# Linear attention gated by an FP4 feed-forward net: the keys' transposes in the pipeline go from TensorE to a DMA, with 16-bit halves split and joined on ScalarE

## The chip, the core and the metric

The kernel runs on one core of a Trainium2 chip. A core has a matrix engine (TensorE, PE in the profile), a vector engine (VectorE, DVE), an engine for activation functions and copies (ScalarE, ACT), a general engine (GpSimd, POOL) and an engine that issues most of this kernel's DMAs (SyncE, SP). They run side by side, each through its own list of instructions in order, and wait for each other by semaphores. Matrix products are written to PSUM, everything else on the chip is in SBUF. The metric is the time of one execution in device microseconds (us); lower is better.

## The reference

`src` has 4 batches of 2048 rows of 256 numbers, all f32. Cut to what is computed:

```python
xn = layernorm(src)                                  # over the 256 numbers of a row
q, k, v = xn @ Wq + bq, xn @ Wk + bk, xn @ Wv + bv   # 16 heads of 64
Q, K = elu(q) + 1, elu(k) + 1
KV = einsum('bshd,bshm->bhdm', K, v)                 # sum over all rows of a batch
Z = 1 / (einsum('bshd,bhd->bsh', Q, K.sum(rows)) + 1e-6)
attn = einsum('bshd,bhdm,bsh->bshm', Q, KV, Z) @ Wo + bo
x1 = layernorm(xn + attn) * g1 + be1
s = layernorm(x1 + gelu(x1 @ W1 + b1) @ W2 + b2) * g2 + be2
h = silu(fp4(xn) @ fp4(w_gate).T) * (fp4(xn) @ fp4(w_up).T)
g = silu(fp4(h) @ fp4(w_down).T)
out = src + s * g
```

`fp4` rounds blocks of 16 numbers to a small grid times a scale of the block. What matters here: KV and the sum of K need all rows of a batch before any of its rows can be finished, and the product for K needs xn with its 256 features on the partitions, that is, transposed.

## The kernel before

Rows are worked in 32 blocks of 256 (T), two tiles of 128 (TB = 2), eight blocks to a batch (NB). The 1024 columns of K are done in two halves of 512, so the keys of a batch are 16 pieces ("subs"): the first eight make the first half, each from one block of rows, and the last eight read the same rows again for the second half.

The keys of batch 0 are done ahead, in a prologue of some 200 us. Then comes the pipeline, the loop over n from line 930: block n of batch b is finished, and two subs of the keys of batch b+1 are done beside it. So in the first four blocks of a batch both subs belong to the first half. For them `keys_in` (line 403) takes the mean and variance, normalizes to xn_k on VectorE and stores it to memory (xn_d); `keys_T` (line 416) calls `keys_xnT` (line 396): four transposes of 128x128 on TensorE into one PSUM tile (pt_k), one copy from there by ScalarE to xnT_k, and a store of that to memory (xnT_d). In the last four blocks of a batch, and for the queries of the block itself, xn and its transpose are read back from there. The last batch has no keys beside it.

One pass of the loop sets this order on TensorE, which is kept as written (lines 97 to 101):

- pt_k of both subs, then pq (the queries, 32 matmuls in four PSUM tiles), pk of the first sub, pz (the denominators), pxk of the first sub (K times xn, summed over the batch), pg (gate and up, for block n+1), pd (down),
- pk of the second sub, pa (attention), pxk of the second sub, most of py (the second feed-forward product of block n-1), pt_x (transposes of x1), pscale, the rest of py, pf (the first feed-forward product of block n).

ScalarE and VectorE have no fixed order in the pipeline (line 916 ends it): a scheduler lays their instructions out when the kernel is built, and SP's too. `tc.issue_after(ins)` puts instructions behind `ins` on their engine. In order of time ScalarE does x1T (from pt_x), scaleT, m_h and m_x (for the fp4 rounding of block n+1), a table load, eight gelus from pf, the two copies of pt_k, the queries' q and e from pq with a table load among them, the keys' two ek, a table load, and the silus of pg.

The keys' chain is in `key_product` and `key_elu` (lines 425 and 440): pk on TensorE, k1 = pk + bias on VectorE, ek = exp on ScalarE, kk on VectorE, and from kk both pxk and, on GpSimd, the sum kacc.

At a block's end `spread_scales` (line 600) sends the fp4 scales by way of memory: scale_d on SP, then eight loads that spread them into qT. `grid_T` (line 617) transposes the fp4 grid, 16-bit numbers, by a DMA on SP (gridT), in two parts of 6 and 10 tiles of 128x128. `quantized_x` and `quantized_h` multiply the two in the next pass. `sums` (line 711) sends the denominators by way of memory (z_d, then four loads zb).

All PSUM tiles of single products share one pool of four ("mm", line 81). In SBUF, "e" has three buffers for the exps, "kk" three for the keys, "xn_k" and "xnT_k" three each.

Of the kernel before, what the change touches and what calls it, by code (L numbers as in the profile page):

```python
# [7 lines left out]

F32 = mybir.dt.float32
BF16 = mybir.dt.bfloat16  # L10
AF = mybir.ActivationFunctionType
ALU = mybir.AluOpType
AX = mybir.AxisListType

P = 128
# [6 lines left out]
def linear_attention_gated_by_fp4_ffn(  # L22
# [34 lines left out]
    nc = tc.nc  # L57
# [5 lines left out]
    ND = D // P  # L63
# [5 lines left out]
    TB = 2  # L69
    T = TB * P  # L70
    NB = S // T
# [6 lines left out]
    work = ctx.enter_context(tc.tile_pool(name="work", bufs=2))  # L78
# [40 lines left out]
    vector, scalar = Ordered(nc.vector), Ordered(nc.scalar)  # L119
# [40 lines left out]
    neg_one = const.tile([P, 1], F32, name="neg_one")  # L160
# [207 lines left out]
    def transposes(x, name):  # L368

        pt = mm_tile(f"pt_{name}").rearrange("p (c t) -> p c t", c=ND)  # L370
        for c in range(ND):
            for j in range(TB):
                tr(
                    pt[:, c, j * P : (j + 1) * P], x[:, j, c * P : (c + 1) * P], ident
                )
        return pt
# [4 lines left out]
    keys = {}  # L381
# [14 lines left out]
    def keys_xnT(n, xn):  # L396
        xnT = work.tile([P, ND, T], F32, tag="xnT_k", name=f"xnT_k_0_{n}", bufs=3)
        scalar.copy(xnT, transposes(xn, f"k_{n}"))
        xnT_d[n] = dram.tile([P, ND, T], F32, tag="xnT_d", name=f"xnT_d_{n}")
        nc.sync.dma_start(xnT_d[n], xnT)  # L400
        return xnT

    def keys_in(b, sub):

        f, bi = divmod(sub, NB)
        n = b * NB + bi
        if f == 0:
            keys[b, sub] = [keys_norm(n, *keys_stats(n))]
        else:
            xn = work.tile([P, TB, D], F32, tag="xn_k", name=f"xn_k_1_{n}", bufs=3)  # L410
            xnT = work.tile([P, ND, T], F32, tag="xnT_k", name=f"xnT_k_1_{n}", bufs=3)
            keys[b, sub] = [xn, xnT]
            nc.sync.dma_start(xn, xn_d[n])
            nc.sync.dma_start(xnT, xnT_d[n])

    def keys_T(b, sub):
        f, bi = divmod(sub, NB)
        if f == 0:
            keys[b, sub].append(keys_xnT(b * NB + bi, keys[b, sub][0]))

    def key_sums(b, f, tag):
        keys[b, "acc", f] = batch.tile([P, HALF], F32, tag="kacc", name=f"kacc_{b}_{f}")
# [2 lines left out]
    def key_product(xnT, f, j, nm):  # L425

        fs = slice(f * HALF, (f + 1) * HALF)
        pk = mm_tile(f"pk_{nm}_{j}")
        for c in range(ND):
            mm(  # L430
                pk, xnT[:, c, j * P : (j + 1) * P], wk_sb[:, c, fs],
                start=c == 0, stop=c == ND - 1,
            )
        k1 = work.tile([P, HALF], F32, tag="q1", name=f"k1_{nm}_{j}", bufs=3)
        vector.tensor_tensor(k1, pk, bk1[:, fs], ALU.add)
        e = work.tile([P, HALF], F32, tag="e", name=f"ek_{nm}_{j}", bufs=3)
        scalar.activation(e, k1, AF.Exp, bias=neg_one)
        return k1, e

    def key_elu(b, f, k1, e, nm, first):  # L440
# [112 lines left out]
    blk = {n: {} for n in range(NBLK)}  # L553
# [77 lines left out]
    def quantized_h(n, j):  # L631

        qh = qT[:, :NI, j * P : (j + 1) * P]
        return vector.tensor_tensor(qh, qh, gridT[n][:, j * NI : (j + 1) * NI, :], ALU.mult)
# [125 lines left out]
    def x1_T(n):  # L760
        x1 = blk[n]["x1"]
        pt = transposes(x1, f"x1_{n}")
        x1T = work.tile([P, ND, T], F32, tag="x1T", name=f"x1T_{n}", bufs=1)
        for c in range(ND):
            ins = scalar.activation(
                x1T[:, c, :], pt[:, c, :], AF.Identity,
                bias=cols["be1"][:, c : c + 1], scale=cols["g1"][:, c : c + 1],
            )
        blk[n]["x1T"] = x1T
        blk[n]["act"] = ins.ins  # L770

        nc.gpsimd.tensor_tensor(x1, x1, rows["g1"], ALU.mult)
        nc.gpsimd.tensor_tensor(x1, x1, rows["shift"], ALU.add)

    def ffn_1(n, chunks=range(NF)):
        x1T = blk[n]["x1T"]
        if "hT" not in blk[n]:
            blk[n]["hT"] = work.tile([P, NF, T], F32, tag="big", name=f"hT_{n}")
        hT = blk[n]["hT"]
        for cc in chunks[::2]:  # L780
            pf = mm_tile(f"pf_{n}_{cc}").rearrange("p (c t) -> p c t", c=2)
            for ci in range(2):
                c = cc + ci
                for d in range(ND):
                    mm(
                        pf[:, ci, :], w1_sb[:, d, c * P : (c + 1) * P], x1T[:, d, :],
                        start=d == 0, stop=d == ND - 1,
                    )
            for ci in range(2):
                c = cc + ci  # L790
                scalar.activation(
                    hT[:, c, :], pf[:, ci, :], AF.Gelu, bias=cols["b1"][:, c : c + 1]
                )

    def ffn_2(n, j, chunks=range(NF)):
        if "py" not in blk[n]:
# [25 lines left out]
    def step(gen, times=1):  # L822
        for _ in range(times):
            next(gen, None)
# [9 lines left out]
    xnT = keys_xnT(0, xn)  # L834
# [95 lines left out]
    for n in range(NBLK):  # L930
        b, bi = divmod(n, NB)
        subs = (2 * bi, 2 * bi + 1) if b + 1 < B else ()
        if n < last:
            gate = gate_up(n + 1)
        for sub in subs:
            keys_T(b + 1, sub)
        if subs:
            step(m_half)
            q_of(n)
            step(down_1)  # L940
            load_xnT(n + 1)
            kk_ins = keys_k(b + 1, subs[0])
            with tc.issue_after(kk_ins):
                ins = quantized_x(n)
            with tc.issue_after(sums(n, ins.ins).ins):
                for j in range(TB):
                    quantized_h(n, j)
            step(m_half)
            keys_xk(b + 1, subs[0])
            step(gate, 9)  # L950
            step(m_half)
            down(n, 0)
            down(n, 1)
        elif n < last:
            def values():
                quantized_h(n, 0)
                return quantized_x(n)

            step(m_half)
            q_of(n, values)  # L960
            quantized_h(n, 1)
            load_xnT(n + 1)
            down(n, 0)
            sums(n)
            step(m_half)
            step(gate, 9)
            step(m_half)
            down(n, 1)
        else:
            for j in range(TB):  # L970
                quantized_h(n, j)
                down(n, j)
        with tc.issue_after(blk[n + 1]["late"]) if n < last else nullcontext():
            qz(n)
        if subs:
            keys_k(b + 1, subs[1])
        elif n > 0:
            ffn_2(n - 1, 0, range(NF // 2))
        attention(n)
        if n + 2 < NBLK:  # L980
            load_xn(n + 2)
        if subs:
            keys_xk(b + 1, subs[1])
            if subs[1] % NB == NB - 1:
                m_half = m_of_half(b + 1, subs[1] // NB)
                step(m_half)
        bn, bin_ = divmod(n + 1, NB)
        next_subs = (2 * bin_, 2 * bin_ + 1) if bn + 1 < B else ()
        for sub in next_subs if n > 0 else ():
            keys_in(bn + 1, sub)  # L990
        if n > 0:
            ffn_2(n - 1, 0, range(0 if subs else NF // 2, NF))
            ffn_2(n - 1, 1, range(NF // 2))
        more = n + 1 < NBLK, n + 2 < NBLK
        if more[0]:
            for j in range(TB):
                scales_h(n + 1, j)
            if more[1]:
                scales_x(n + 2)
        for sub in next_subs if n == 0 else ():  # L1000
            keys_in(bn + 1, sub)
        x1_T(n)

        half_way = NF // 2 if subs else 3 * NF // 4
        if n > 0:
            ffn_2(n - 1, 1, range(NF // 2, half_way))
        if more[0]:
            spread_scales(n + 1, *more)
        if n > 0:
            ffn_2(n - 1, 1, range(half_way, NF))  # L1010
        if more[0]:
            grid_of_h(n + 1, 0)
            grid_T(n + 1, 0, NI)
            grid_of_h(n + 1, 1, blk[n]["act"])
            if more[1]:
                grid_of_x(n + 2, blk[n]["act"])
            grid_T(n + 1, NI, (NCH if more[1] else NI) * TB)
        if n > 0:
            output(n - 1)
        if n + 1 == last:  # L1020
            q_of(last)
            ffn_1(n, range(NF // 2))
            sums(last)
            ffn_1(n, range(NF // 2, NF))
        else:
            ffn_1(n)
    for j in range(TB):
        ffn_2(last, j)
        output(last, [j])
# [34 lines left out]
```

## Time and profile before

| | |
|---|---|
| median of 3 runs | 1939.84 us (1937.8 to 1939.91) |
| the profiled execution: its time, its span | 1942.96 us, 1941.1 us |
| TensorE clock granted | 0.997 |
| busy: PE, DVE, ACT, POOL | 1918.2, 1276.6, 765.2, 534.9 us |
| matmuls of pt_k: all, after 215 us | 128, 80 |
| table loads on ScalarE | 122, 156.5 us |
| DMA queue of SP: packets, data, share of the 16 DMA engines | 200008, 178.22 MB, 42.8% |

The profile is of one execution. Its span begins with the first instruction and ends with the last, and the time of the execution includes what lies around it. Durations of single instructions are latencies: matmuls overlap, so the time that a group of them holds TensorE is read from the chain of waits in order of time (start, length, engine, tile, count) and not from the mean of one. In rows of the timeline the columns are start, length, engine, line, operation, output<-inputs, shapes, count, and in brackets the idle time before and what ended it. Instructions of VectorE and ScalarE carry line 114, that of the helper that issues them, so they are told apart by their tiles.

### The profile page before, as it was taken

What the parts mean: (1) busy time and instruction counts of PE and PEld (TensorE: products, weight loads), DVE (VectorE), ACT (ScalarE), POOL (GpSimd) and SP (SyncE); (2) the same over time, 40 slices, a digit from 0 to 9 for tenths busy, and PEclk for the clock granted to TensorE, in tenths of its full rate; (3) what the DMA queues carried; (4) which work ended last, traced back from release to release, by engine and by line L of the source; (5) the groups of instructions that cost most, each with busy time, mean ns of one, the idle gap of its engine ahead of it and who ended that gap; (6) DMA issues with size and microseconds to landing.
All of it is one profiled execution on the core that took longest, in us unless ns stands there. A gap on an engine that the chain in (4) does not pass through costs nothing.

```text
span 1941.1 us, 22716 instructions
## 1 busy us (share of the span) xinstructions
PE 1918.2 (99%) x8108; PEld 1381.0 (71%) x8108; DVE 1276.6 (66%) x2300; ACT 765.2 (39%) x1340; POOL 534.9 (28%) x455
## 2 busy tenths in 40 slices
PE   9999999999999999999999999999999999999998
PEld 4446677667777677777677776677776778787786
DVE  6878656666566666666666666666565676777763
ACT  2334444334443344443343433444433443344442
POOL 4431232322233222322222323222232212222212
PEclk9999999999999999999999999999999999999999
DMA  4435445344435345444443442454533444444541
GB/s 149 144 98 120 100 93 118 83 105 91 91 59 106 94 85 107 112 91 96 89 86 71 105 104 83 89 113 93 100 80 73 75 81 86 86 82 85 90 82 41
DMA packets 200953, 181.23 MB, mean 93 GB/s; under 512 B 80101, under 2 KB 161537, under 8 KB 200841
## 3 DMA queue, kind: packets, MB, share of 16 engines
q1 hardware_dynamic: 200008, 178.22, 42.8%
q10 hardware_dynamic: 832, 1.57, 0.2%
q8 instruction: 64, 1.05, 0.2%
q14 instruction: 49, 0.39, 0.1%
HBM read 131.41 MB, written 31.54 MB: 84 GB/s over the span
## 4 chain that ended last, share of the span: by engine, by line
PE 87%; DVE 1%; DMA 1%; issue 1%; SPq 0%; POOL 0%; ACT 0%; POOLq 0%; DVEq 0%
PE pg L98 15%; PE pa L98 11%; PE pf L98 11%; PE pq L98 11%; PE py L98 11%; PE pxk L98 8%; PE pk L98 8%; PE pd L98 8%; PE pz L98 2%; PE pt_x L101 1%; PE pm L98 1%; PE pt_k L101 0%; PE pkv L98 0%; DMA zb<-z_d 0%; PE pks L98 0%
## 5 line engine op out<-in xcount | busy, mean ns | idle before, releaser
L98 PE MATMUL pg<-wgu,qT 128*128 128x352 f32 x1024 | 310.4, 461 | 0.0
L98 PEld LDWEIGHTS pg<-wgu,qT 128*128 128x128 f32 x1024 | 193.2, 190 | 118.6 <-issue 13.9
L448 POOL TENSOR_TENSOR kacc<-kacc,kk 128x512 f32<-128x512 f32 x120 | 171.8, 1432 | 298.4 <-DVE kk L114 296.4
L98 PE MATMUL pxk<-kk,xn_k 128*128 128x512 f32 x512 | 235.5, 599 | 3.3 <-DVE kk L114 3.3
L98 PE MATMUL py<-w_sb,hT 128*128 128x256 f32 x1024 | 234.5, 380 | 0.5 <-DVE s L114 0.5
L98 PE MATMUL pk<-wk_sb,xnT_k 128*128 128x512 f32 x512 | 232.1, 596 | 1.8 <-ACT xnT_k L114 1.5
L98 PE MATMUL pa<-m,zq 128*128 128x256 f32 x1024 | 228.3, 381 | 3.0 <-DVE zq L114 3.0
L98 PE MATMUL pq<-xnT,wq_sb 128*128 128x256 f32 x1024 | 228.1, 381 | 0.0
L98 PE MATMUL pf<-x1T,w_sb 128*128 128x256 f32 x1024 | 226.6, 379 | 0.0
L98 PEld LDWEIGHTS pa<-m,zq 128*128 128x128 f32 x1024 | 195.2, 191 | 41.3 <-issue 12.3
L98 PEld LDWEIGHTS py<-w_sb,hT 128*128 128x128 f32 x1024 | 191.1, 190 | 37.9 <-issue 8.1
L98 PEld LDWEIGHTS pq<-xnT,wq_sb 128*128 128x128 f32 x1024 | 194.8, 191 | 26.6 <-ACT hT L114 0.3
L98 PEld LDWEIGHTS pf<-x1T,w_sb 128*128 128x128 f32 x1024 | 194.3, 190 | 27.0 <-ACT hT L114 0.4
L677 POOL TENSOR_TENSOR o<-g,be_r 128x512 f32<-128x512 f32 x32 | 44.9, 1404 | 578.7 <-ACT g L114 578.7
L114 ACT ACT_TABLE_LOAD x122 | 156.5, 1283 | 87.1 <-DVE k L114 73.9
L114 ACT ACTIVATE x1T<-pt_x,bcol 128x256 f32<-128x256 f32 x64 | 32.6, 559 | 358.5 <-PE pt_x L101 358.5
L98 PE MATMUL pd<-wd,qT 128*128 128x256 f32 x768 | 172.3, 379 | 0.5 <-DVE qT L114 0.5
L98 PEld LDWEIGHTS pk<-wk_sb,xnT_k 128*128 128x128 f32 x512 | 97.6, 191 | 104.6 <-issue 97.0
L98 PEld LDWEIGHTS pxk<-kk,xn_k 128*128 128x128 f32 x512 | 92.5, 190 | 108.7 <-issue 80.8
L114 DVE SCALAR_TENSOR_TENSOR zq<-e,q 128x512 f32<-128x512 f32 x128 | 87.1, 689 | 124.8 <-ACT e L114 124.6
L98 PEld LDWEIGHTS pd<-wd,qT 128*128 128x128 f32 x768 | 145.8, 190 | 24.8 <-DVE qT L114 1.2
L358 POOL TENSOR_TENSOR rstd<-rstd,neg_half 128x2 f32<-128x2 f32 (+1 forms) x97 | 72.8, 751 | 316.9 <-DVE rstd L114 269.8
(121 smaller groups left out, 2324.7 us busy)
## 6 DMA issues: line engine op xcount, KB each, us to landing
zb<-z_d SPq DMA_DIRECT2D x128, 256.0 KB, 6.3
qT<-scale_d SPq DMA_DIRECT2D x248, 128.0 KB, 5.5
x_k<-in_L_attn_src_dram SPq DMA_DIRECT2D x32, 256.0 KB, 2.9
x<-in_L_attn_src_dram SPq DMA_DIRECT2D x32, 256.0 KB
xn_d<-xn_k SPq DMA_DIRECT2D x32, 256.0 KB, 3.2
xn<-xn_d SPq DMA_DIRECT2D x32, 256.0 KB, 2.6
xnT_d<-xnT_k SPq DMA_DIRECT2D x32, 256.0 KB, 5.0
xnT<-xnT_d SPq DMA_DIRECT2D x32, 256.0 KB, 2.7
```

What stands on the lines that cost most here:

```text
L98: return tc.keep_in_program_order(nc.tensor.matmul(*args, **kw))
L101: return tc.keep_in_program_order(nc.tensor.transpose(*args, **kw))
L114: ins = op(*args, **kw)
L358: nc.gpsimd.tensor_tensor(rstd[:, j0:j1], rstd[:, j0:j1], neg_half[:, j0:j1], ALU.pow)
L448: nc.gpsimd.tensor_tensor(kacc, kacc, kk, ALU.add)
L677: nc.gpsimd.tensor_tensor(o, g, rows["be2"], ALU.mult)
```

## The change

In the pipeline, from block 1 on, the keys' xn is transposed by a DMA. The DMA transpose that the kernel has, of 16-bit numbers, is used on the two halves of each f32:

- `keys_apart` sees xn_k as 16-bit numbers. Two copies on ScalarE, one for each half, of 512 numbers a partition read every second 16-bit number and write them together into `apart` (a buffer of "e"). One DMA on SP transposes its 8 tiles of 128x128 into `apartT` (a buffer of "kk").
- `keys_T` then joins them: one ScalarE copy of 1024 16-bit numbers, from apartT into xnT_k, seen as 16-bit numbers, so that each write goes to every second one. The store to xnT_d follows as before.

The places: both subs' `keys_apart` are at the end of the block before, the first one's ahead of `x1_T(n)`, the second one's behind x1T's activations. The first sub's joining is behind the last gelu of `ffn_1(n)`; the second's is moved into the next block, behind the first sub's exps. The two subs of the first block keep TensorE's transposes. The prologue is not changed.

```diff
     def keys_xnT(n, xn):
         ...
         scalar.copy(xnT, transposes(xn, f"k_{n}"))
+        store_xnT(n, xnT)
+        return xnT
+
+    def store_xnT(n, xnT):
         xnT_d[n] = dram.tile([P, ND, T], F32, tag="xnT_d", name=f"xnT_d_{n}")
         nc.sync.dma_start(xnT_d[n], xnT)
-        return xnT
...
+    def keys_apart(b, sub, issue=None):
+        f, bi = divmod(sub, NB)
+        if f > 0:
+            return
+        n = b * NB + bi
+        half = keys[b, sub][0].bitcast(U16).rearrange("p j (c f h) -> p h c j f", c=ND, h=2)
+        apart = work.tile([P, 2, ND, TB, P], U16, tag="e", name=f"apart_{n}", bufs=3)
+        with tc.issue_after(issue) if issue is not None else nullcontext():
+            for h in range(2):
+                scalar.copy(apart[:, h], half[:, h])
+        apartT = work.tile([P, 2, ND * T], U16, tag="kk", name=f"apartT_{n}", bufs=3)
+        nc.sync.dma_start(
+            apartT.rearrange("p h (m t) -> p (h m) t", t=P),
+            apart.rearrange("p h c j f -> p (h c j f)"),
+            transpose=True,
+        )
+        keys[b, sub].append(apartT)
+
-    def keys_T(b, sub):
+    def keys_T(b, sub, issue=None):
         f, bi = divmod(sub, NB)
-        if f == 0:
-            keys[b, sub].append(keys_xnT(b * NB + bi, keys[b, sub][0]))
+        if f > 0:
+            return
+        n = b * NB + bi
+        xn, *apartT = keys[b, sub]
+        xnT = work.tile([P, ND, T], F32, tag="xnT_k", name=f"xnT_k_0_{n}", bufs=3)
+        if apartT:
+            with tc.issue_after(issue):
+                scalar.copy(
+                    xnT.bitcast(U16).rearrange("p c (t h) -> p h (c t)", h=2), apartT[0]
+                )
+        else:
+            scalar.copy(xnT, transposes(xn, f"k_{n}"))
+        store_xnT(n, xnT)
+        keys[b, sub] = [xn, xnT]
...
-        scalar.activation(e, k1, AF.Exp, bias=neg_one)
+        keys["exp"] = scalar.activation(e, k1, AF.Exp, bias=neg_one).ins
...
-        for sub in subs:
+        for sub in subs if n == 0 else ():
             keys_T(b + 1, sub)
...
                 for j in range(TB):
                     quantized_h(n, j)
+            if n > 0:
+                keys_T(b + 1, subs[1], keys["exp"])
             step(m_half)
...
+        for sub in next_subs[:1]:
+            keys_apart(bn + 1, sub)
         x1_T(n)
+        for sub in next_subs[1:]:
+            keys_apart(bn + 1, sub, blk[n]["act"])
...
             ffn_1(n)
+        for sub in next_subs[:1]:
+            keys_T(bn + 1, sub, blk[n]["gelu"])
```

`ffn_1` also keeps its last gelu as `blk[n]["gelu"]`, and `blk[n]["act"]` is x1T's second activation, as before.

More of the change, by code (lines that the diff above doesn't have):

```diff
@@ L10 @@
 BF16 = mybir.dt.bfloat16
+U16 = mybir.dt.uint16
 AF = mybir.ActivationFunctionType
@@ L790, in ffn_1 @@
                 c = cc + ci
-                scalar.activation(
+                ins = scalar.activation(
                     hT[:, c, :], pf[:, ci, :], AF.Gelu, bias=cols["b1"][:, c : c + 1]
                 )
+        blk[n]["gelu"] = ins.ins
     def ffn_2(n, j, chunks=range(NF)):
```

## The prediction

> **What bounds the kernel now.** I read the page first (busy shares, then the chain of waits by engine), then the chain in order of time around single blocks.
>
> ```profile
> PE 1918.2 (99%) x8108; PEld 1381.0 (71%) x8108; DVE 1276.6 (66%) x2300; ACT 765.2 (39%) x1340; POOL 534.9 (28%) x455
> ...
> PE 87%; DVE 1%; DMA 1%; issue 1%; SPq 0%; POOL 0%; ACT 0%; POOLq 0%; DVEq 0%
> ```
>
> TensorE is busy 99% of the span and the chain is TensorE: the time is its list of matmuls, run nearly without a gap. So the question is how much list the change takes away, and where a gap opens. The chain in time, first a block whose end still has the keys' transposes (pt_k), then one that has none, because its keys' xnT is read back from memory:
>
> ```profile
> 263.63 6.91 PE pf L98 x32
> 270.54 0.87 PE pt_k L101 x8
> 271.41 6.91 PE pq L98 x32
> ```
> ```profile
> 442.76 6.91 PE pf L98 x32
> 449.67 6.91 PE pq L98 x32
> 456.57 3.43 PE pk L98 x8
> 460.00 1.00 PE pz L98 x16
> 461.01 3.63 PE pxk L98 x8
> ```
>
> With transposes pf to pq is 7.78 us, without them 6.91: eight transposes cost **0.87 us**, 109 ns each. The second block also shows that pq can follow pf directly: it is the changed kernel's order, already running. And its pxk takes 3.63 us where the block's other pxk takes 3.43 in the chain: this join (pk, VectorE's k, ScalarE's ek, VectorE's kk, pxk) already waits 0.2 us, so ScalarE running late there is paid in full.
>
> **Removed.** The pipeline transposes at the ends of blocks 0-2, 7-10 and 15-18: 11 times two tiles of four, 88 transposes. Here the view of the tile pt_k (duration min/median/max; these 80 are those after the first block, 8 more are the first block's) tempts to a larger sum:
>
> ```profile
> L101 PE MATMUL pt_k<-ident,xn_k x80: 272/273/273, 270.4 to 1277.3; 128*128 128x128 f32 x80
> L114 ACT COPY xnT_k<-pt_k x20: 584/596/607, 271.3 to 1277.9; 128x512 f32<-128x512 f32 x20
> ```
>
> 88 x 273 ns = 24.0 us. The Trainium skill says the same (TensorE: Matmul & The Clock Gate, Part 4: PE-mode transpose: about 275 ns for one in a kernel's context). But that is the latency of one; they overlap, and the chain has 0.87 us for eight. By row and rule the time would fall to 1915.8, by the chain 11 x 0.87 = **9.6 us**. I take the chain: its two differences (7.78 and 6.91) measure what TensorE is kept from. Also gone are 22 ScalarE copies of 0.6 us from PSUM, and two PSUM tiles a block.
>
> **Added on ScalarE**, per tile: two splitting copies of 512 numbers and one recombining copy of 1024. No row of before shows 16-bit copies at a stride. The nearest read SBUF and write 16 bits:
>
> ```profile
> L114 ACT ACTIVATE m_h<-h 128x704 bf16<-128x704 f32 x64 | 50.9, 796 | 46.9 <-DVE h L114 46.9
> ...
> L114 ACT ACTIVATE m_x<-y 128x512 bf16<-128x512 f32 x32 | 20.2, 632 | 5.7 <-DVE rstd L114 2.6 <-DVE y L114 2.5
> ```
>
> Slope (796-632)/192 = 0.85 ns a number: a split 0.63 us, a recombination 0.63 + 512 x 0.85 = **1.07 us**. The recombination writes every second 16-bit slot and the splits read so. Lower end: as the rows (1.07); upper end, if each half-written word costs double or more, 2.1 to 3.2 us, 2 to 3 times the row. The Trainium skill bears on it (SBUF — State Buffer, Door 1, the note on cachelines): access is at full rate while at least two accesses fall in one 16-byte line, and each step to a new line is penalised. A step of 4 bytes has four accesses in a line, so by that rule there is no penalty; no row here shows one way or the other. I take 1.07. In total ScalarE gets 22 x (2 x 0.63 + 1.07 - 0.60) = 38 us, on 765 of 1941: only its places matter.
>
> *First tile's recombination* is behind the last gelu of ffn_1. Queued behind it are the q's, whose exps feed zq, pz and the tight join. ScalarE in the block without transposes:
>
> ```profile
> 449.70 0.84 ACT L114 ACTIVATE hT<-pf,bcol 128x256 f32<-128x256 f32 x2 [0.89 <-PE pf L98]
> 451.43 0.84 ACT L114 ACTIVATE q<-pq,bcol 128x256 f32<-128x256 f32 x2 [0.89 <-PE pq L98]
> ...
> 457.88 0.72 ACT L114 ACTIVATE e<-q,neg_one 128x512 f32<-128x512 f32 x1
> 459.05 0.72 ACT L114 ACTIVATE ek<-k,neg_one 128x512 f32<-128x512 f32 x1 [0.45 <-DVE k L114]
> 461.13 0.72 ACT L114 ACTIVATE ek<-k,neg_one 128x512 f32<-128x512 f32 x1 [1.36 <-DVE k L114]
> ```
>
> Between gelu (ends 450.54) and q lie 0.89 us, and consecutive copies overlap by 0.1 us (before, two of 0.6 took 1.07). So about 1.0 us is free; from there to the last e ScalarE has no gap, and then 0.45 us before ek. A recombination up to about 1.1 + 0.45 = **1.55 us costs nothing**; every further us is a us of TensorE. At 1.07: nothing. Before, the two old copies sat there at 1.07 us as well.
>
> *Second tile's recombination* is behind the block's first two ek. Behind it wait the next table load (1.28 us) and the silu of pg. In the first block shown ScalarE idles 2.7 us there: 1.07 fits; without that cover, 1 us a block through pg's PSUM tiles.
>
> *First tile's splits* are ready when xn_k is (317 us in the block that ends at 320), in an idle stretch of 14.3 us before x1T: nothing. *Second tile's splits* come after x1T's activation, ahead of scaleT, m_h, m_x, table load and gelus: at most 1.26 us later. The first gelu would be at 325.4 instead of 324.15; TensorE needs that PSUM tile for the first pq at 329; the later gelus have 0.89 us of idle time each, so it is caught up. VectorE's grid work slips by the same 1.26 us into the 4.1 us it idles before the first zq. Nothing.
>
> **Added on SP and the DMA engines:** 22 transposes. The rows:
>
> ```profile
> L621 SPq DMA_TRANSPOSE gridT<-grid x63: 1225/1277/1967, 163.2 to 1884.9; - x63
> ...
> DMA to landing us min/median/max: 2.7/6.2/7.9
> ```
>
> New ones have 8 tiles of 128x128, the old 6 and 10: 1.3 us of issue, 2.7 (DMA engines quiet) to 7.9 us (busy) to land. First tile: copies done at 318.3, landed by 327.5 at worst, used at 329. Second: used some 20 us later. On SP the second transpose stands ahead of scale_d, 8 qT loads and the gridT transpose, and waits for the splits: scale_d goes about 2.7 us later, plus at most 1.5 us on the DMA engines. gridT, issued at 327.3 and landed by about 333.5, comes by 337.7; it is first used at 342.9, now 342.0. Hidden with 4 us to spare. The change of batch (blocks 7 and 15) has its ksum load among these too: VectorE waits 4.1 us for it until 618.06; 2.5 us more leaves some 0.6 of the 3.1 us it idles before zq: hidden, just. The second xnT_d store moves from SP's place at 331 to about 343, ahead of z_d and the four zb; zb then lands up to 1 us later, and attention has 5 us. Shared buffers (e, kk) are free in time: apart is read before the next q's, apartT goes with the recombination.
>
> **The first block** is the exception: no ffn_2 lies before ffn_1, the first gelu starts at 210.17, 4 us after its pf tile, and xn_k of the second tile is ready only at 211.6. If its splits are ahead of the gelus (208.9), these slip 2.7 + 1.26 = 4.0 us, once; if behind, some 0.7 in front of q. I take 0.7; ends 0 and 4.
>
> **Sum.** 9.6 - 0.7 = 8.9 us. The profiled execution has span 1941.1 and time 1942.96 us, so 1934.1 for a like execution; from the median of the runs, 1939.84 - 8.9 = **1931.0 us**. Within 0.2% (3.9 us) a measurement can't be told from no change.
>
> **Rivals.**
> - *The recombination is dear* (the slower side). One place: between gelu and q, 11 times. Free to 1.55 us, even at 1.55 + 8.9 / 11 = 2.4 us. At twice the row (2.14) it stalls 0.59 x 11 = 6.5 us: 1937.5. At three times (3.2) 1.65 x 11 = 18.2 us: 1949.2. For it: no row of such a copy, and the tight pxk. Against: the rows with 16-bit output keep one slope. 22%.
> - *The gain is given back by waits:* ScalarE's and SP's queues come out in another order than I laid, and a gelu, q or qT product stands 0.5 to 0.9 us a block. 11 x 0.7 = 7.7 us lost: 1938.7. For it: the order isn't written out past the named places. Against: 3 to 14 us of cover at most of them. 15%.
> - *The row's price holds:* 24 us gone, 1915.8. Against: the chain. 3%.
> - *Forecast:* 60%, its own range 1929 to 1936.
>
> Faster 0.63, same 0.15, slower 0.22. The range 1927 to 1946 takes in the first block's ends, a recombination up to some 2.9 us, and leaves out the dear end (about 0.13) and the row's price (0.03).
>
> **What would show it.** Right: pf to pq at 6.91 us in all 11 blocks, 88 transposes fewer, recombination near 1.07 us, pxk still 3.63 us. Wrong: a recombination over 1.55 us, q starting late behind it with pz and pxk longer (rival one); an idle ScalarE in front of a recombination, waiting for its DMA, or qT's product behind its loads (rival two).

## The result and the profile after

The changed kernel takes 1933.49 us (median of 9 runs, 1931.66 to 1936.48), the kernel before, run beside it, 1939.84: 6.35 us less, a ratio of 0.9966 with a 95% interval of 0.9956 to 0.9977. Two later measurements gave 0.9965 (0.9952 to 0.9977) and 0.9971 (0.9959 to 0.9983). The forecast was 8.9 us less.

The page of the changed kernel, the lines that answer to those shown of before:

```profile
PE 1906.7 (99%) x8020; PEld 1369.5 (71%) x8020; DVE 1270.7 (66%) x2300; ACT 802.9 (42%) x1384; POOL 534.5 (28%) x455
...
PE 84%; DMA 2%; DVE 1%; ACT 1%; SPq 1%; issue 0%; POOL 0%; POOLq 0%; DVEq 0%; ACTq 0%
```

88 matmuls fewer (8108 to 8020), ScalarE 38 us busier (765.2 to 802.9), TensorE as full as before. The chain's share on TensorE is 84% for 87%: in the first block the chain now runs 23 us over other engines (none before), and from block 23 on it stands on DMAs for 34 us, before for 14; in the 22 blocks between it is on TensorE alone, both times. The chain in order of time around the end of block 1, where before 0.87 us of pt_k stood between pf and pq:

```profile
263.85 6.91 PE pf L99 x32
270.76 6.91 PE pq L99 x32
277.66 3.43 PE pk L99 x8
281.10 1.00 PE pz L99 x16
282.10 3.63 PE pxk L99 x8
```

pq follows pf at once, and pk, pz and pxk have the lengths of before to the hundredth: the transposes are gone and no wait took their place. The same over the whole stretch from block 1's pf to that of block 23 (columns: stretch, length, then busy time and count of PE, PEld, DVE, ACT and POOL, TensorE's clock, DMA share, GB/s), first before, then the change:

```profile
263.60:1564.70 1301.10, 1301.10 (x5508) 940.73 (x5507) 825.77 (x1510) 522.41 (x908) 356.08 (x291) 1.00 0.44 92
```
```profile
263.80:1556.10 1292.30, 1292.30 (x5428) 932.56 (x5427) 823.20 (x1510) 555.50 (x945) 354.55 (x291) 1.00 0.46 97
```

TensorE is busy in all of it, both times; the stretch is shorter by 8.8 us for 80 matmuls fewer, 110 ns each.

So the 6.35 us are a sum of unlike parts. The start of each block's pf, read from the traces, divides the time into four stretches; the table, in us, is the key to all that follows:

| kernel | start to block 0's pf | to block 1's pf | to block 22's pf | to the end |
|---|---|---|---|---|
| before | 204.4 | 59.1 | 1242.2 | 435.5 |
| before, again | 204.5 | 59.1 | 1242.1 | 432.4 |
| the change | 203.3 | 60.4 | 1233.4 | 432.8 |
| the change, again | 203.0 | 60.4 | 1233.4 | 433.8 |
| the change, third | 202.9 | 60.4 | 1233.4 | 433.6 |

The two middle columns are the same to 0.1 us in each profile of a kernel: the first block 1.3 us longer, the 21 after it 8.8 us shorter, together some **7.4 us less** (ratio 0.9962, in all three intervals). The outer columns hold work that the change leaves alone. The last one differs by 3 us between two profiles of the same kernel. The first one, with the first loads, repeats to 0.4 us in the profiles of a kernel, but lies anywhere from 202.3 to 205.5 us in the kernels below, which do the same work up to there. The 1.1 to 1.6 us by which the change is ahead in it are there before any changed instruction runs (the second pt_k starts at 22.9 us in the one profile and at 21.8 in the other); what makes them, and whether every execution has them, is not settled. In the first pair of profiles, 11.2 us apart, both outer columns were on the change's side; the medians lie 0.3 to 1.7 us short of 7.4.

### The profile page after: what moved, and what is told of

It is laid out like the page before. It is cut to its first block, busy times and chain, and to the rows that moved or that the text cites. A ratio compares the mean times of both kernels' runs of the same rounds, so it can differ in the third digit from the quotient of the medians.

```text
span 1929.9 us, 22642 instructions
## 1 busy us (share of the span) xinstructions
PE 1906.7 (99%) x8020; PEld 1369.5 (71%) x8020; DVE 1270.7 (66%) x2300; ACT 802.9 (42%) x1384; POOL 534.5 (28%) x455
## 3 DMA queue, kind: packets, MB, share of 16 engines
q8 instruction: 63, 1.03, 0.2%
## 4 chain that ended last, share of the span: by engine, by line
PE 84%; DMA 2%; DVE 1%; ACT 1%; SPq 1%; issue 0%; POOL 0%; POOLq 0%; DVEq 0%; ACTq 0%
PE pg L99 15%; PE py L99 11%; PE pa L99 11%; PE pf L99 10%; PE pq L99 10%; PE pxk L99 8%; PE pk L99 8%; PE pd L99 8%; PE pz L99 2%; DMA qT<-scale_d 1%; PE pt_x L102 1%; PE pm L99 1%; SPq L648 0%; DVE zq L115 0%; DMA zb<-z_d 0%
```

## The experiments

**The scatter: both kernels once more**, without an edit.

> The kernel before, once more, for its own scatter: ratio 1.000 within 0.1%. The profile of before took 376.4 us from the pf of block 22 to the end, that of the change 373.9, though the change leaves those blocks alone. If that is scatter between executions, this profile's last blocks lie anywhere from 373 to 377 us, and blocks 1 to 22 take 1301.1 us again.

> The changed kernel once more. By the chain of its profile blocks 1 to 22 take 1292.3 us (8.8 less) and the stretch up to block 1's pf 0.2 us more, so the whole should be 8.6 us less: ratio 0.9956. If something gives back 2 us in every execution (as the first median, 6.35 us less, would have it), the ratio is 0.9966 and one of the three stretches is longer than in the first profile of the change.

Measured: before against itself 1.0001 (0.9993 to 1.0009); the change 1932.28, 7.1 us under before on the same chip, ratio 0.9965. The last stretch of before came out 3.1 us shorter with not an instruction changed, so the 2.7 us that the first pair of profiles showed there are no part of the change. In the second profile of the change the last stretch is 1.0 us longer than in its first, which is within that scatter, and the first 0.3 us shorter. The first block has its 1.3 us in each: that is the part of the forecast that failed, and three experiments below go after it.

**What removing alone brings.** In the kernel before, for all tiles of the pipeline but those of block 0, the transposes are left out, and ScalarE's copy takes xn_k as it lies:

```diff
-            keys[b, sub].append(keys_xnT(b * NB + bi, keys[b, sub][0]))
...
+            scalar.copy(xnT.rearrange("p c t -> p (c t)"), xn.rearrange("p j d -> p (j d)"))
...
```

> The kernel before without the 88 transposes and with nothing in their place: ScalarE copies xn_k to xnT_k as it lies, so the keys of batches 1 to 3 are made from rows that are not transposed. No splits, no DMA transposes, no 16-bit joining. If a transpose holds TensorE for 109 ns (the chain), 9.6 us less than before: 1930.3, ratio 0.9951. If it holds it for its 273 ns (the row), 24 us less: 1915.8, ratio 0.988. If TensorE then waits for something else, under 5 us less.

Measured: 1929.1 us, ratio 0.9952 (0.9940 to 0.9965), 10.3 less. First block 57.9 us, the next 21 1233.4: 1.2 + 8.8 = 10.0 us by the chain. The row's price (24 us) is out. The changed kernel's 21 blocks take exactly what they take here, with a plain copy of 0.62 us in place of splits, DMA and joining: there all the added work costs nothing.

**The added work alone.** In the changed kernel TensorE's transposes are put back at their old place, read by nothing:

```diff
+        for sub in subs if n > 0 and bi < NB // 2 else ():
+            transposes(keys[b + 1, sub][0], f"k_{b}_{sub}")
```

> The changed kernel with TensorE's 88 transposes put back in their old places, into PSUM tiles that nothing reads: the added work alone. By the chain's price the changed kernel plus 9.6 us, so 1.1 us more than before (the first block's loss): 1941, ratio 1.0005. By the row's price the changed kernel plus 24: 1957, ratio 1.009. If the added ScalarE work and transposes on SP cost something in every block that the removal hides, more than 1941 by that, with pf to pq over 7.78 us or pxk over 3.63 us in the chain.

Measured: 1942.26 us, ratio 1.0016 (1.0008 to 1.0024), 9.98 us over the changed kernel in the same session: 113 ns for each of 88. Its chain in order of time, at the place shown before:

```profile
263.68 6.91 PE pf L99 x32
270.59 0.87 PE pt_k L102 x8
271.46 6.91 PE pq L99 x32
278.37 3.43 PE pk L99 x8
281.81 1.00 PE pz L99 x16
282.81 3.63 PE pxk L99 x8
```

These are the numbers of before, with splits, DMA transposes and joinings running beside: 1242.1 us for the 21 blocks, as before. Only the first block is longer, 61.2 us for 59.1: the added work costs 2.1 us, all of it there. (The 1.1 us expected was the first block's loss less what the removal gains there.) The median has 2.9 us more than before; 0.8 of that no stretch of its one profile shows, and that profile is of the shortest of its 15 runs.

**How far the joining was from costing.** The rival that would have made the change slower was a dear joining. What the added operations took, in the view of groups by form (mean ns of one after the busy time), and the view of the DMA's tile (duration min/median/max, and time to landing):

```profile
L115 ACT COPY xnT_k<-apartT 128x1024 uint16<-128x1024 uint16 x22 | 29.4, 1335 | 0.0
L115 ACT COPY apart<-xn_k 128x512 uint16<-128x512 uint16 x44 | 25.0, 617 | 89.3 <-DVE mv L115 88.7 <-DVE xn_k L115 0.6
```
```profile
L432 SPq DMA_TRANSPOSE apartT<-apart x22: 1231/1250/1892, 207.6 to 1262.4; - x22
...
DMA to landing us min/median/max: 3.1/3.5/4.0
```

The splits are as forecast (0.617 for 0.63), the joinings a quarter dearer (1.335 for 1.07), and ScalarE never sat idle in front of a joining (0.0): no joining waited for its DMA. ScalarE's timeline at the end of block 2 shows what that left:

```profile
328.55 0.84 ACT L115 ACTIVATE hT<-pf,bcol 128x256 f32<-128x256 f32 x2 [0.89 <-PE pf L99]
329.27 1.34 ACT L115 COPY xnT_k<-apartT 128x1024 uint16<-128x1024 uint16 x1
330.47 0.84 ACT L115 ACTIVATE q<-pq,bcol 128x256 f32<-128x256 f32 x2
...
337.89 0.72 ACT L115 ACTIVATE ek<-k,neg_one 128x512 f32<-128x512 f32 x1 [0.26 <-DVE k L115]
```

q no longer waits for TensorE, it waits for the joining; the idle time before ek is 0.26 us, where the block without transposes had 0.45. With 1.55 us free and 1.33 used, 0.22 was to be left. Then the joining of each first tile was made twice:

```diff
-                scalar.copy(
-                    xnT.bitcast(U16).rearrange("p c (t h) -> p h (c t)", h=2), apartT[0]
-                )
+                for _ in range(2 - sub % 2):
+                    scalar.copy(
+                        xnT.bitcast(U16).rearrange("p c (t h) -> p h (c t)", h=2), apartT[0]
+                    )
```

> The changed kernel with the first tile's joining copy made twice, 11 copies more. A joining took 1.33 us and ScalarE still idled 0.26 us before ek. If ScalarE's queue between the last gelu and ek is free up to about 1.55 us and costs TensorE one for one beyond it, two joinings (2.57 us, as neighbours overlap by 0.1) cost 2.57 - 1.33 - 0.26 = 1.0 us a block, 11 us in all: 1943, ratio 1.002, with pz or pxk longer by 1.0 us in the chain. If ScalarE isn't on the way there, 1932 as the changed kernel.

Measured: 1945.09 us, ratio 1.0028 (1.0018 to 1.0037): slower than before. The 21 blocks take 1243.7 us, 10.3 more for ten second joinings; the first block 1.5 more. The mean, 1.03 us, is the 1.0 that was worked out, but no block shows it: eight are 1.16 to 1.17 us longer, and the two at a change of batch (7 and 15) 0.51, for there 32 small matmuls (pkv, 1.15 us) stand between pz and pxk and take up part of the delay. So the agreement of the mean is in part luck. The chain in block 2, which in the changed kernel runs on TensorE alone here, now leaves it between pf and pxk (lines in order of time):

```profile
333.31 1.23 ACT xnT_k L115
334.54 0.33 ACT q L115
334.87 1.23 ACT xnT_k L115
336.10 0.70 ACT q L115 x2
336.81 1.28 ACT L115
...
340.89 0.62 ACT e L115
...
342.14 0.55 DVE k L115
...
343.43 0.23 DVE k L115
...
343.94 0.69 DVE kk L115
344.68 3.88 PE pxk L99 x8
```

TensorE's timeline at this place, first in the changed kernel, then here:

```profile
338.78 1.07 PE L99 MATMUL pz<-zq,kh 128*32 128x256 f32 x16
339.78 3.70 PE L99 MATMUL pxk<-kk,xn_k 128*128 128x512 f32 x8
```
```profile
342.70 1.40 PE L99 MATMUL pz<-zq,kh 128*32 128x256 f32 x16
344.68 3.88 PE L99 MATMUL pxk<-kk,xn_k 128*128 128x512 f32 x8 [0.57 <-DVE kk L115]
```

This is what a joining twice as dear could have looked like. The delay goes through q and e on ScalarE and then over VectorE, which must finish its zq before it turns to k, and from k to kk. It comes out as 0.33 us in pz, a gap of 0.57 us where pz and pxk overlapped by 0.07, and 0.18 us in pxk: 1.15 us. The room that ran out is VectorE's: its k waited 0.28 us for pk in the changed kernel and comes straight behind a zq here, while ScalarE still idles 0.24 us before ek. The kernel is also not the changed one and a copy alone, for the scheduler laid the neighbours out anew: a q stands between the two joinings, and VectorE's second k ahead of the first kk. What is shown is that 1.33 us of joining cost nothing and 2.57 cost 1.16 in eight of ten blocks. If each further us costs one, the joining is free up to some 1.4 us, not 1.55; where the limit lies was not measured.

**Why the joining was dearer.** The same copy, turned so that it writes side by side and reads in turn from the two halves:

```diff
-                    xnT.bitcast(U16).rearrange("p c (t h) -> p h (c t)", h=2), apartT[0]
+                    xnT.bitcast(U16).rearrange("p c (t h) -> p (c t) h", h=2),
+                    apartT[0].rearrange("p h m -> p m h"),
```

> The changed kernel with the joining's order turned: it writes 16-bit numbers side by side and reads them in turn from the two halves of apartT, 1024 bytes apart. The joining took 1.33 us where the rows of before gave 1.07. If the writes at every second 16-bit number make the 0.26 us, 1.07 us now; if a read that jumps to another place costs more, over 1.33. The time stays the changed kernel's as long as a joining is under 1.55 us: 1932.

The view of its tile:

```profile
L115 ACT COPY xnT_k<-apartT x22: 1145/1152/1197, 216.3 to 1283.3; 128x1024 uint16<-128x1024 uint16 x22
```

1.15 us for 1.33. Reading at every second number costs nothing: the splits take 617 ns each, and a plain f32 copy of as many numbers, in the kernel without the transposes, takes 619:

```profile
L114 ACT COPY xnT_k<-xn_k 128x512 f32<-128x512 f32 x22 | 13.6, 619 | 104.6 <-DVE xn_k L114 104.6
```

The turned copy differs from the joining in its writing and in its reading, so the 0.18 us between them are the price of writing every second 16-bit number, less the price, if any, of reading in turn from 1024 bytes apart: the writing costs at least 0.18. Of the 0.26 us that were missing from the estimate of 1.07 the other 0.08 stay open. The time is the same (1932.93 us, 0.9967, interval 0.9956 to 0.9979; 21 blocks 1233.5), as it must be when the joining of 1.33 us already costs nothing.

**The cover of the DMAs.** Each transpose issued twice into the same place, so that SP also waits for the first to land:

```diff
+        for _ in range(2):
             nc.sync.dma_start(
                 apartT.rearrange("p h (m t) -> p (h m) t", t=P),
...
```

> The changed kernel with each tile's DMA transpose issued twice into the same place: twice the load on SP and the DMA engines, and SP waits for the first to land (some 3.5 us) before it issues the second. If the transposes are hidden with 4 us to spare before qT's product, as forecast, scale_d and the qT loads come 2.5 to 5 us later and blocks 1 to 22 are 0 to 1 us a block longer: 1932 to 1943. If there is no such cover, each block is longer by the whole 2.5 to 5 us: 1960 or more.

Measured: 1934.11 us, ratio 0.9976 (0.9966 to 0.9986); the 21 blocks take 1233.4 us, not a tenth more. SP's timeline at the end of block 2, whose pf starts at 324.38 here:

```profile
324.83 2.61 SPq L433 DMA_TRANSPOSE apartT<-apart x2
327.54 0.65 SPq L646 DMA_DIRECT2D scale_d<-scaleT  x1
329.50 1.23 SPq L433 DMA_TRANSPOSE apartT<-apart  x1
330.83 3.85 SPq L649 DMA_DIRECT2D qT<-scale_d  x8
335.15 1.33 SPq L658 DMA_TRANSPOSE gridT<-grid  x1
```

The scheduler put scale_d between the two, so it is softer than planned: gridT is issued 10.8 us after pf, against 8.0 in the changed kernel (pf at 321.60) and 5.0 before (pf at 322.26):

```profile
329.57 1.36 SPq L657 DMA_TRANSPOSE gridT<-grid  x1
```
```profile
327.26 1.34 SPq L621 DMA_TRANSPOSE gridT<-grid  x1
```

Its product with qT starts at 344.1 all the same, 19.7 us after pf as in the changed kernel, straight behind kk. So the changed kernel's 3.0 us of delay on this queue are hidden with at least 2.8 to spare. The first block is 1.2 us longer (61.6); the joining stands behind the first of the queries' e there, in another order than the changed kernel's.

**The first block.** Before, the chain was on TensorE there, and pq came 8.1 us after the start of pf, the transposes included:

```profile
204.43 7.19 PE pf L98 x32
211.62 0.87 PE pt_k L101 x8
212.49 0.02 issue
212.52 7.17 PE pq L98 x32
```

What happens in the changed kernel, on ScalarE and then on TensorE:

```profile
208.16 1.28 ACT L115 ACT_TABLE_LOAD   x1
209.45 0.47 ACT L115 ACTIVATE hT<-pf,bcol 128x256 f32<-128x256 f32 x1
210.56 1.14 ACT L115 COPY apart<-xn_k 128x512 uint16<-128x512 uint16 x2 [0.64 <-DVE xn_k L115]
211.61 2.65 ACT L115 ACTIVATE hT<-pf,bcol 128x256 f32<-128x256 f32 x7
214.11 1.37 ACT L115 COPY xnT_k<-apartT 128x1024 uint16<-128x1024 uint16 x1
```
```profile
203.33 7.20 PE L99 MATMUL pf<-x1T,w_sb 128*128 128x256 f32 x32
212.13 7.17 PE L99 MATMUL pq<-xnT,wq_sb 128*128 128x256 f32 x32 [1.60 <-ACT hT L115]
```

The second tile's splits stand between the first gelu and the other seven; they wait 0.64 us for xn_k and take 1.14. pq needs the PSUM tile of the first two gelus, so TensorE waits 1.60 us for the second one, and pq comes 8.8 us after pf. Behind it pz and pxk take 0.2 and 0.4 us longer than before. Two kernels undo parts of it. First, TensorE's transposes again for the first block's two tiles:

```diff
-        for sub in subs if n == 0 else ():
+        for sub in subs if n < 2 else ():
             keys_T(b + 1, sub)
...
-        for sub in next_subs[:1]:
+        for sub in next_subs[:1] if n > 0 else ():
             keys_apart(bn + 1, sub)
...
```

> The changed kernel with the two tiles at the first block's end transposed by TensorE as before (10 blocks by DMA in place of 11). From the first block's pf to the second's took 59.1 us before, 60.4 with the change and 57.9 where the transposes were left out and nothing put in. If the splits and joinings in ScalarE's late stretch are what costs 2.2 us there, it is 59.1 again: 1.3 us under the changed kernel, 1931, ratio 0.9958.

The first block takes 59.1 us again, as expected. The median, 1934.5 us (0.9971, interval 0.9961 to 0.9982), doesn't show it: in its profile the last stretch took 437.0 us, the longest of all here. Second, the second tile later, and its joining between the silus:

```diff
-            if n > 0:
+            if n == 1:
+                keys_apart(b + 1, subs[1], keys["exp"])
+            elif n > 1:
                 keys_T(b + 1, subs[1], keys["exp"])
...
             step(gate, 9)
+            if n == 1:
+                keys_T(b + 1, subs[1], blk[n + 1]["silu"])
...
```

> The changed kernel with the second tile of the first block's end split later, behind the next block's first ek, and joined between its silus; the first tile as in the change. If it is the second tile's splits ahead of the gelus that cost (they waited for xn_k, and a pq waited 1.6 us for a gelu), the first block takes 58.3 to 58.8 us in place of 60.4: 1930.5, ratio 0.9955. If the first tile's joining costs as much, no better than 59.5.

58.6 us for the first block: 1.8 of the 2.2 us are back, so it was the second tile's splits. ScalarE has no gap there from the table load to the first ek; the first tile's splits put the gelus 0.4 us later (6.1 us after pf, before 5.75), and the joining takes the place of the two old copies. That these hold the rest was not tried by itself. The median is 1933.07 us (0.9965, interval 0.9953 to 0.9977), again no less than the change's.

**Both gains together**, and the changed kernel a third time beside them:

> The changed kernel with both small gains together: the first block's second tile split and joined later (58.6 us for the first block in place of 60.4) and the joining that writes side by side (1.15 us in place of 1.33). By the chain 1.8 to 2 us under the changed kernel: 58.4 to 58.6 us for the first block, 1930.5 in all. The first loads and the last eight blocks scatter by 1 to 3 us between executions, so the medians may not show it.

> The changed kernel beside the other two on the same chip: 7.4 us less than before by its chain without the first loads (8.75 less in blocks 1 to 22, 1.3 more in the first block): ratio 0.9962. The first block 60.4 us again, the stretch to the first pf and the last blocks free to lie 1 to 3 us off.

Measured: 1930.75 us, ratio 0.9959 (0.9946 to 0.9971); the changed kernel in the same session 1933.07, ratio 0.9971 (0.9959 to 0.9983). First block 58.4 us, the 21 blocks 1233.4. By the chain 1.9 us under the change, by the medians 2.3, but the intervals overlap: the gain is seen in the trace and not proved by the times. It is the version I would keep.

## Why the prediction was right, and where it was off

*The price of a transpose.* Taken from the chain, 0.87 us for eight, against 273 ns in the row and about 275 in the Trainium skill (TensorE: Matmul & The Clock Gate, Part 4: PE-mode transpose; its figure is for bf16, these are f32). Shown by both experiments on it: 10.3 us less with the transposes out, 9.98 more with them back in. Row and page agree on how long one transpose lasts; a sum made from them would have been 2.5 times too large.

*No new wait in the blocks.* Shown: 1233.4 us for the 21 blocks in the change and without transposes, splits and joinings. Pf to pq is 6.91 us in ten of the 11 blocks, not in all; the first has 8.8.

*The joining* was mis-sized, 1.07 for 1.33, and the Trainium skill's note on cachelines (SBUF — State Buffer, Door 1), by which a step of 4 bytes is free, holds for the reads measured and not for the writes (at least 0.18 us more). It made no difference, because the price up to which it is free had been worked out beside it. That price, 1.55 us, is right in kind and not confirmed in size: the doubled joining, in another order of instructions, fits 1.4 us in eight blocks. It does show the slower rival to be a real one: with 1.2 us more of ScalarE's time at this place the kernel is slower than before.

*The queue on SP.* Forecast: gridT up to 4.2 us late with 4 to spare. It came 3.0 late, and 2.8 more cost nothing.

*The first block* is the step that failed, as a term that was mis-sized: "if behind, some 0.7 in front of q. I take 0.7; ends 0 and 4." It cost 2.2 us (60.4 for 59.1 less 0.87). The order was neither of the two laid: the splits came between the first gelu and the second. The first tile's splits, put at nothing everywhere, also hold up the gelus there by 0.4 us. With 2.2 for 0.7 the sum is 7.4, and the medians' 5.7 to 7.1 are that and the scatter of the outer stretches. Whether the changed kernel also loses some tenths in the unprofiled runs stays open; no profile shows a place. They would be more if those runs have its shorter first stretch too.

*Rivals.* Row's price: out. Gain given back by waits: not in the 21 blocks; the first block gave back 2.2 of 9.6. Dear joining: not reached.

## What to carry to other kernels

Take the price of work on a full engine from how much longer its chain is with the work than without, not from the duration of one instruction: overlapped transposes here cost 110 ns and last 273. For work moved to an engine with time to spare, what counts is how late each new instruction may be at its place; two such numbers (more than 1.33 us before ek, at least 5.8 us before qT's product) decided this change, and the mean load (42%) said nothing. Compare block by block before a mean is taken for a confirmation: the doubled joining's 1.03 us is made of 1.16 and 0.51. Look at the first pass through a loop by itself: its covers are other than those of the passes after it.

## What the hardware showed unexpectedly

A ScalarE copy of 1024 16-bit numbers takes 1.33 us when it writes every second one and 1.15 when it writes them side by side and reads in turn from two places; 512 read at every second place take 0.617, no more than a plain copy of 512 f32 numbers (0.619). A DMA transpose of eight 128x128 tiles landed in 3.1 to 4.0 us at the blocks' ends, where the forecast had allowed up to 7.9, and doubling it cost nothing in 21 blocks. With the same instructions, the last stretch of before took 435.5 and 432.4 us: two single profiles of this kernel can differ by 3 us where nothing was changed.
